# A four-layer graph kernel: layer 2 in the natural order of rows, and 18 of layer 3's gather slots joined into six

## The chip, the cores and the metric

The kernel runs on one core of one Trainium2 chip. The metric is the device time of one execution in microseconds (us); lower is better. Before the change the median of three runs is 708.24 us (708.03 to 709.66).

## The reference

Four graph layers work on one feature matrix `x` (2708 rows of 128 numbers, float32) and one sparse adjacency matrix `adj` (2708 x 2708, the same for all). Each layer adds its result to `x` and normalises every row:

```python
x = layernorm(x + layer0(x, adj))   # signed attention
x = layernorm(x + layer1(x, adj))   # relu(D^-1/2 (A + I) D^-1/2 (x W^T + b))
x = layernorm(x + layer2(x, adj))   # softmax over neighbours; entries below 1 are masked by (adj - 1) * 1e9
x = layernorm(x + layer3(x, adj))
# layer 3, for all i, j:
#   messages[i, j] = gelu(x_i Ws + x_j Wd + b);  agg_i = sum_j adj[i, j] * messages[i, j]
#   h = gelu([x_i, agg_i] Wu + bu) + x_i;  then a row norm with weights
```

Because of the mask, layer 2 needs of every row only its own (diagonal) entry and its largest neighbour. Layer 3 needs all non-zero neighbours of a row: up to some twenty, most rows far fewer.

## The kernel before, in words

The 2708 rows are 22 blocks of 128 (`NB`), one row per partition. While layers 0 and 1 run as dense products on TensorE (PE), VectorE (DVE) finds the non-zero entries of each row: their values in `V[row, block, slot]`, largest first, and their columns, from which `LIDX` is made. For that, rows are put into *places*: sorted by their number of neighbours, most first. `PERM` gives the row of a place, `RANK` the place of a row. `CAPS` gives how many slots a block of places has, from 21 down to 2, 187 in all. So a block with a large cap is one in which a few rows need many slots.

**Layer 1** (`half_of`, L740, with `finish`, L628) multiplies block after block. A chunk of four blocks is finished in small steps (`yield`) that are laid between the products of the next: transposes, residual and sums (DVE, L641 and L649), squares (ScalarE, ACT, L257), three small steps on GpSimd (POOL, L261 to L263), norm (L267), transposes, projection for layer 2 (L678, L684). Then the block goes to DRAM twice: as `TA` in the order of rows (L687, one plain DMA per chunk) and as `TS` in the order of places (L693, one indirect DMA by `RANK` for each block, on POOL). In the last stretch (L781 to L803) the steps still open are driven on after each product, by `if layer or m % 2` (L786). `in_order_of_rows` (L505) turns a vector in the order of places into the order of rows by 22 small matmuls; it is used for `dinv` in layer 1 (L892).

**Layer 2** (L908 to L1081) works on places, in four sets of 6, 6, 6 and 4 blocks. POOL gathers each place's largest neighbour from `TA` into `ga` (L918, 22 indirect DMAs), SP loads the places' own rows from `TS` into `OWN` (L922). For each set, `own_scores`, `shares` and `rows2` run mostly on DVE, `squares` on ACT with a product on PE, `roots` on DVE; `rows3` makes `yd`, what a row gives as a neighbour in layer 3, and scatters it to `TD` in the order of rows (L1052, 22 indirect DMAs on POOL; `yd` has two buffers). `norm3` writes the rows themselves into `X3` (L1061), all sets at the end. In the loop of L1070, `roots` and `rows3` of a set come one set later than its `squares`.

**Layer 3** (L1087 on) takes the 22 blocks of places in the order `TURN`. For turn k: `gathers` (L1150) fetches one slot of 128 neighbours from `TD` with each indirect DMA, into `G` (four buffers); `terms` makes x Ws + b on PE; `messages` adds (DVE, L1179) and applies gelu (ACT, L1180 and L1181); `diagonals` makes for every slot a diagonal matrix of the weights `V` (ACT, L1171); `update` multiplies message by diagonal and sums over slots in PSUM (PE, through `product`, L1143), then the update product and gelu (L1196); `added` and `norms` finish rows on DVE (L1206, L1217 to L1241); `stores` scatters them to the output (L1250, indirect DMA on POOL). Ahead of turn 0, `conditions` (L1099) tests whether the lists are complete and sets the flag that would call a dense path.

The order is written out by hand: `pinned` (L210) ties an instruction to the one pinned before it on the same engine. The DMAs of SP and ACT and the output stores are not pinned.

```python
def pinned(i):
    e = i.ins.engine
    if e in newest:
        tc.add_manual_dep(i.ins, newest[e].name, ..., reason="order")
    newest[e] = i.ins
    return i
```

Of the kernel before, what the change touches and what calls it, by code (L numbers as in the profile page):

```python
# [24 lines left out]
F32 = mybir.dt.float32  # L25
# [4 lines left out]
U32 = mybir.dt.uint32  # L30
# [20 lines left out]
TABLE = (("kk", 32), ("lane", 128), ("part", 1), ("lt", 128), ("ident", 128))  # L51


def table():
# [9 lines left out]
        "ident": p == np.arange(P),  # L64
    }
# [4 lines left out]
def sparse_path(  # L70
# [64 lines left out]
    TAB = const.tile([P, sum(w for _, w in TABLE)], F32, name="TAB")  # L135
    nc.scalar.dma_start(TAB, consts)
    part, at = {}, 0
    for name, w in TABLE:
        part[name] = TAB[:, at : at + w]
        at += w  # L140
# [62 lines left out]
    PERMF = const.tile([P, NB], F32, name="PERMF")  # L203

# [97 lines left out]
    def parts(dst, src, pool, n):  # L302

        rest = pool.tile([P, n], F32, name=f"rest{n}")
        nc.vector.tensor_copy(dst[:, :, 0], src)
        nc.vector.tensor_tensor(rest, src, dst[:, :, 0], ALU.subtract)
        nc.vector.tensor_copy(dst[:, :, 1], rest)
        nc.vector.tensor_tensor(rest, rest, dst[:, :, 1], ALU.subtract)
        nc.vector.tensor_copy(dst[:, :, 2], rest)
# [195 lines left out]
    def in_order_of_rows(ps, dst, src):  # L505

        s3 = small.tile([P, NB, 3], BF16, name="back3")
        parts(s3, src, small, NB)
# [89 lines left out]
    TS = dram.tile([NP, W_], F32, name="TS")  # L598
    H2 = lists.tile([P, NB, D], F32, name="H2")
    with (  # L600
# [27 lines left out]
        def finish(layer, bs, sT):  # L628
# [40 lines left out]
            if layer:  # L669
# [21 lines left out]

                for b in bs:
                    i = G_.indirect_dma_start(  # L693
                        TS, bass.IndirectOffsetOnAxis(ap=RANK[:, b : b + 1], axis=0),
                        XD[:, b, :], None,
                    )
                    tc.declare_no_dep(i.ins, group="TS", reason="each row has a place of its own")
                    tc.add_to_no_dep_group("TS", i.ins)
# [41 lines left out]
        def half_of(layer, h, weights, each, end, later):  # L740
# [40 lines left out]
            for i, c in enumerate(half):  # L781
                for m, (n, a) in enumerate(last):
# [3 lines left out]
                    if layer or m % 2:  # L786
                        for g in drain:
                            next(g, None)
# [79 lines left out]
        EARLY = 4  # L868
        for k in range(4):
            features(k)  # L870
        given(range(EARLY))
        weights(0)
        for h in range(2):

            def each1(n, a, lo, hi, h=h):
                if h:
                    return
# [28 lines left out]
    OWN = late.tile([P, NB, W_], F32, name="OWN")  # L906
    X3 = late.tile([P, NB, D], F32, name="X3")
    with (  # L908
# [6 lines left out]
        for k, bs in enumerate(sets):  # L915
            ga = gas[k] = one.tile([P, len(bs), D + HEADS], F32, name=f"ga{k}")
            for i, b in enumerate(bs):
                pinned(G_.indirect_dma_start(  # L918
                    ga[:, i, :], None, TA, bass.IndirectOffsetOnAxis(ap=LIDX[:, b, 0:1], axis=0)
                ))  # L920
        for k, bs in enumerate(sets):
            nc.sync.dma_start(  # L922
                OWN[:, bs[0] : bs[-1] + 1, :],
# [875 lines left out]
```

## Time and profile before

| what | value |
|---|---|
| median of three runs | 708.24 us |
| the profiled execution, its own time | 709.3 us |
| its span, first to last instruction | 707.5 us |
| mean granted TensorE clock | 0.766 |
| busy: PE, DVE, ACT, POOL | 451.2, 393.0, 272.4, 378.5 us |
| layer 3's gathers L1150 (POOL) | 187, mean 948 ns |
| layer 2's gathers L918 (POOL) | 22, mean 1075 ns |
| TS scatters L693, TD scatters L1052 (POOL) | 22 and 22, means 982 and 1102 ns |

The profile is one execution. A line of a timeline gives the start in us from the span's start, the duration, the engine, the line of the program, the operation with out<-in, and in brackets how long the engine sat idle before it and what ended that. A line of the costliest groups gives the busy time and the mean in ns, then the idle time before them with what ended most of it. "issue" is time for which the profile shows no wait. The digits of an engine's row in the part with 40 slices are tenths of busy time, each slice being 17.7 us. [...]

### The profile page before, as it was taken

Reading aid. Unit: us, or ns where it says so; the run is one execution under the profiler, and the core shown is the slowest. Engines: PE = TensorE matmul, PEld = TensorE weight load, DVE = VectorE, ACT = ScalarE, POOL = GpSimd, SP = SyncE. Lnnn points to the kernel's source line nnn. Section 1 sums busy time; section 2 is a strip of 40 time slices with the busy share of each in tenths; the row PEclk is TensorE's granted clock in tenths of the full one; section 3 lists DMA queues with packets and bytes.
Section 4 is the critical chain, followed back from the end, with each engine's and each line's share of the span. In section 5 each row is a group of like instructions: output and inputs, shape, how many; then the busy total and the mean of one; then the engine's idle time right before and its main releaser. Section 6 shows DMA issues by size and latency. Waiting matters only on the chain.

```text
span 707.5 us, 8193 instructions
## 1 busy us (share of the span) xinstructions
PE 451.2 (64%) x2565; PEld 301.7 (43%) x2565; DVE 393.0 (56%) x1138; ACT 272.4 (38%) x719; POOL 378.5 (53%) x449
## 2 busy tenths in 40 slices
PE   5889999996164999997511502066646546747461
PEld 5745445663152444464311501055536435545451
DVE  4767999999983856640208834111171251434466
ACT  3145655772330100174411574055335424444330
POOL 7002001221246776036577677777777777777761
PEclk9579999998556999999755555566776857788665
DMA  9968999996294999875254111222122122211210
GB/s 296 406 245 309 415 415 379 324 374 224 101 386 153 419 418 415 311 216 191 85 181 128 42 52 40 53 54 52 52 53 55 53 53 53 53 52 52 54 48 13
DMA packets 44400, 128.68 MB, mean 182 GB/s; under 512 B 7983, under 2 KB 19523, under 8 KB 38716
## 3 DMA queue, kind: packets, MB, share of 16 engines
q0 software_dynamic: 16832, 75.13, 30.2%
q1 hardware_dynamic: 21116, 49.66, 19.7%
q10 hardware_dynamic: 6400, 3.29, 1.7%
q8 instruction: 22, 0.36, 0.2%
q14 instruction: 30, 0.25, 0.1%
HBM read 119.29 MB, written 8.81 MB: 181 GB/s over the span
## 4 chain that ended last, share of the span: by engine, by line
DVE 27%; POOL 24%; PE 19%; issue 14%; DMA 9%; ACT 6%; SPq 0%; POOLq 0%; DVEq 0%; ACTq 0%
POOL G L1150 17%; PE acc L753 12%; DVE IX L580 9%; DVE cand L565 5%; DMA G<-TD,LIDX 4%; PE z L753 3%; POOL ga L918 2%; DMA TOP<-in_high 1%; POOL TS L693 1%; ACT squares L257 1%; PE w_ps L355 1%; ACT XD L267 1%; ACT X L1061 1%; DMA nat<-in_adjo,PERM 1%; POOL ln_r L262 1%
## 5 line engine op out<-in xcount | busy, mean ns | idle before, releaser
L1150 POOL DMA_INDIRECT G<-TD,LIDX x187 | 177.4, 948 | 58.7 <-issue 52.4
L1143 PE MATMUL aT_ps<-W,M 128*128 128x128 f32 x418 | 91.0, 394 | 112.5 <-ACT M L1180 105.1
L1143 PEld LDWEIGHTS aT_ps<-W,M 128*128 128x128 f32 x418 | 80.9, 292 | 126.4 <-ACT M L1180 114.0
L1179 DVE TENSOR_TENSOR M<-G,sd_ps 128x1152 f32<-128x1152 f32 (+11 forms) x22 | 28.3, 1287 | 159.0 <-DMA G<-TD,LIDX 142.8
L753 PE MATMUL acc<-ah,XD 128*128 128x512 f32 (+1 forms) x264 | 113.7, 568 | 1.0 <-ACT XD L626 1.0
L580 DVE FIND_INDEX8 IX<-V,nat 128x8 uint32<-128x2707 f32 x33 | 97.8, 2970 | 0.0
L830 ACT ACTIVATE sign<-ah 128x1536 bf16<-128x1536 f32 (+1 forms) x44 | 57.7, 1327 | 37.1 <-issue 26.8
L753 PE MATMUL acc<-ah,HS 128*128 128x512 f32 x132 | 63.3, 615 | 12.1 <-ACT HS L866 12.1
L753 PEld LDWEIGHTS acc<-ah,XD 128*128 128x128 f32 x264 | 47.9, 196 | 44.5 <-issue 41.4
L536 POOL DMA_INDIRECT nat<-in_adjo,PERM x22 | 21.5, 979 | 81.5 <-DVE IX L580 55.4
L1171 ACT ACTIVATE W<-TAB,V 128x128 f32<-128x128 f32 x187 | 56.8, 390 | 0.0
L558 DVE MAX8 V<-nat 128x8 f32<-128x2707 f32 x12 | 35.7, 2976 | 26.6 <-DMA nat<-in_adjo,PERM 26.6
L1180 ACT ACTIVATE M<-sd_ps 128x128 f32<-128x128 f32 x22 | 6.1, 278 | 113.2 <-DVE M L1179 113.2
L753 PEld LDWEIGHTS acc<-ah,HS 128*128 128x128 f32 x132 | 25.4, 196 | 44.7 <-issue 29.3
L866 ACT ACTIVATE HS<-HS,DS 128x128 f32<-128x128 f32 x22 | 8.4, 399 | 78.0 <-DMA HS<-TH,PERM 48.8
L565 DVE MAX8 cand<-nat 128x8 f32<-128x338 f32 (+3 forms) x88 | 34.3, 461 | 2.8 <-DMA nat<-in_adjo,PERM 2.8
L251 POOL TENSOR_SCALAR ln_a<-SUM 128x4 f32<-128x4 f32 (+1 forms) x12 | 2.9, 238 | 61.1 <-DVE XD L649 33.2
L1250 POOL DMA_INDIRECT out_x<-yo,PERM x22 | 22.1, 1003 | 18.5 <-DVE yo L1229 11.3
L861 POOL DMA_INDIRECT HS<-TH,PERM x22 | 21.0, 957 | 19.6 <-DMA TH<-H 10.1
L1052 POOL DMA_INDIRECT TD<-yd,PERM x22 | 24.2, 1102 | 9.6 <-ACT yd L1048 4.1
L753 PE MATMUL acc<-ah,H 128*128 128x512 f32 (+1 forms) x88 | 28.1, 462 | 0.0
L693 POOL DMA_INDIRECT TS<-XD,RANK x22 | 21.6, 982 | 11.3 <-issue 5.4
(281 smaller groups left out, 862.6 us busy)
## 6 DMA issues: line engine op xcount, KB each, us to landing
ah<-in_adjL SPq DMA_DIRECT2D x22, 768.0 KB, 13.5
ah<-in_adjR SPq DMA_DIRECT2D x44, 330.0 KB, 5.5
TOP<-in_high SPq DMA_DIRECT2D x5, 1354.0 KB, 13.0
ah<-in_adjL SPq DMA_DIRECT2D x22, 256.0 KB, 7.2
G<-TD,LIDX POOLq DMA_INDIRECT x187, 2.5
OWN<-TS SPq DMA_DIRECT2D x3, 798.0 KB, 8.5
TA<-XD ACTq DMA_DIRECT2D x5, 264.0 KB, 2.8
TH<-H ACTq DMA_DIRECT2D x5, 256.0 KB, 10.2
```

The source lines that it names most:

```text
L558: pinned(nc.vector.max(V[:, b, 0:8], t))
L565: pinned(nc.vector.max(c[:, 8 * k : 8 * k + 8], t[:, at]))
L580: pinned(nc.vector.max_index(IX[:, b, s], V[:, b, s], t))
L693: i = G_.indirect_dma_start(TS, bass.IndirectOffsetOnAxis(ap=RANK[:, b : b + 1], axis=0), XD[:, b, :], None,)
L753: pinned(T_.matmul(acc[i][:, :w], weights[:, n, :], a[:, i * BANK : i * BANK + w], start=n == 0, stop=n == NB - 1,))
L830: pinned(S_.activation(m[:, : hi - lo], a, AF.Sign))
L1052: i = G_.indirect_dma_start(TD, bass.IndirectOffsetOnAxis(ap=PERM[:, b : b + 1], axis=0), yd[:, i, :], None)
L1143: pinned(T_.matmul(t, a, b, start=n == 0, stop=n == len(parts) - 1))
L1150: pinned(G_.indirect_dma_start(G[:, s, :], None, TD, bass.IndirectOffsetOnAxis(ap=LIDX[:, b, s : s + 1], axis=0),))
L1171: pinned(S_.activation(W[:, s, :], ident, AF.Copy, scale=V[:, b, s : s + 1]))
L1179: pinned(V_.tensor_tensor(M[:, :n, :], G[:, :n, :], s_, ALU.add))
L1250: i = G_.indirect_dma_start(out, bass.IndirectOffsetOnAxis(ap=PERM[:, b : b + 1], axis=0), h, None, bounds_check=N - 1, oob_is_err=False,)
```

## The change

Layer 2 now works on rows in their natural order. `OWN` is the tile `XD` that layer 1 leaves in SBUF; `TS`, its scatters and its load are gone. The two vectors that layer 2 needs of the lists, the largest neighbour's value (`V1`) and its column (`J1`), are brought into the order of rows by `in_order_of_rows` in the second half of layer 1, at blocks 5 and 9. `TD` is written by a plain DMA on SP for each set. What layer 3 needs in the order of places (the rows, the diagonal and the count: 130 numbers) is scattered by `RANK` to `XS` (`to_places`, 22 indirect DMAs on POOL, pinned) and read back into `X3S` (`from_places`, four DMAs on SP). In layer 2's loop `roots` and `rows3` follow the `squares` of the same set. In layer 1's last stretch the open steps are not driven on during the last, short chunk.

In layer 3, 18 slots that few rows use are joined into six groups (`JOINED`: block, slot, number of rows). Each group is one gather of at most 128 rows (`joined_gathers`), with a message step of its own; its indices and weights are collected by 36 small DMAs on SP (`joined_lists`). In `update` a block uses its piece of a group through a shifted part of the identity. `FULL` is what is left of `CAPS`: 169 slots, none in block 21. `conditions` counts with a mask (`uses`). The `XJ` memset is on DVE. In `messages` the own row's gelu now comes ahead of DVE's add.

```diff
@@ -48,7 +48,42 @@
 CAPS = (21, 13, 12, 11, 11, 10, 10, 9, 9, 9, 8, 8, 8, 7, 7, 6, 6, 6, 5, 5, 4, 2)
-TABLE = (("kk", 32), ("lane", 128), ("part", 1), ("lt", 128), ("ident", 128))
+JOINED = (
+    ((2, 11, 97), (0, 16, 23), (0, 20, 8)),
+    ((1, 12, 85), (0, 15, 41)),
+    ((0, 14, 65), (17, 5, 62)),
+    ((20, 3, 68), (19, 4, 48), (9, 8, 12)),
+    ((6, 9, 56), (4, 10, 41), (0, 17, 14), (0, 18, 10)),
+    ((12, 7, 40), (21, 0, 26), (21, 1, 22), (0, 19, 9)),
+)
+FULL = tuple(
+    min([c] + [s for q in JOINED for b, s, _ in q if b == k]) for k, c in enumerate(CAPS)
+)
+PARTS = tuple(
+    tuple(
+        (q, sum(m for *_, m in g[:i]), n)
+        for q, g in enumerate(JOINED)
+        for i, (b, _, n) in enumerate(g)
+        if b == k
+    )
+    for k in range(len(CAPS))
+)
+def used(b, s):
+    if s >= CAPS[b]:
+        return 0
+    return next((n for g in JOINED for k, t, n in g if (k, t) == (b, s)), P)
...
                     TA[bs[0] * P : (bs[-1] + 1) * P, :].rearrange("(b p) c -> p b c", p=P),
                     XP[:, g, : D + HEADS],
                 )
...
-                for b in bs:
-                    i = G_.indirect_dma_start(
-                        TS, bass.IndirectOffsetOnAxis(ap=RANK[:, b : b + 1], axis=0),
-                        XD[:, b, :], None,
-                    )
-                    tc.declare_no_dep(i.ins, group="TS", reason="each row has a place of its own")
-                    tc.add_to_no_dep_group("TS", i.ins)
...
@@ -783,7 +814,7 @@
                     product(n, a, i)
                     if not layer:
                         search(0.28)
-                    if layer or m % 2:
+                    if m % 2 if not layer else c != NC - 1:
                         for g in drain:
                             next(g, None)
...
             def each1(n, a, lo, hi, h=h):
                 if h:
+                    if n == 5:
+                        in_order_of_rows(pt, V1, V[:, :, 0])
+                    if n == 9:
+                        pinned(V_.tensor_copy(JF, LIDX[:, :, 0]))
+                        in_order_of_rows(pt, JS, JF)
+                        pinned(V_.tensor_copy(J1, JS))
                     return
...
+    USES = late.tile([P, NB, SLOTS], F32, name="USES")
+    nc.sync.dma_start(USES.rearrange("p b s -> p (b s)"), consts[:, W_TAB:])
+    NJ = len(JOINED)
+    LJ = late.tile([P, NJ], U32, name="LJ")
+    VJ = late.tile([P, NJ], F32, name="VJ")
+    nc.gpsimd.memset(LJ, 0)
+    nc.gpsimd.memset(VJ, 0.0)
+    def joined_lists():
+        for q, g in enumerate(JOINED):
+            at = 0
+            for b, s, n in g:
+                nc.sync.dma_start(LJ[at : at + n, q : q + 1], LIDX[:n, b, s : s + 1])
+                nc.sync.dma_start(VJ[at : at + n, q : q + 1], V[:n, b, s : s + 1])
+                at += n
+    OWN = XD
+    X3N = late.tile([P, NB, D + 2], F32, name="X3N")
+    X3S = late.tile([P, NB, D + 2], F32, name="X3S")
+    X3 = X3S[:, :, :D]
+    XS = dram.tile([NP, D + 2], F32, name="XS")
+    def to_places(bs):
+        for b in bs:
+            i = pinned(G_.indirect_dma_start(
+                XS, bass.IndirectOffsetOnAxis(ap=RANK[:, b : b + 1], axis=0), X3N[:, b, :], None
+            ))
+            tc.declare_no_dep(i.ins, group="XS", reason="each row has a place of its own")
+            tc.add_to_no_dep_group("XS", i.ins)
+    def from_places():
+        for bs in groups(6):
+            nc.sync.dma_start(
+                X3S[:, bs[0] : bs[-1] + 1, :],
+                XS[bs[0] * P : (bs[-1] + 1) * P, :].rearrange("(b p) c -> p b c", p=P),
+            )
...
             ga = gas[k] = one.tile([P, len(bs), D + HEADS], F32, name=f"ga{k}")
             for i, b in enumerate(bs):
                 pinned(G_.indirect_dma_start(
-                    ga[:, i, :], None, TA, bass.IndirectOffsetOnAxis(ap=LIDX[:, b, 0:1], axis=0)
+                    ga[:, i, :], None, TA, bass.IndirectOffsetOnAxis(ap=J1[:, b : b + 1], axis=0)
                 ))
-        for k, bs in enumerate(sets):
-            nc.sync.dma_start(
-                OWN[:, bs[0] : bs[-1] + 1, :],
-                TS[bs[0] * P : (bs[-1] + 1) * P, :].rearrange("(b p) c -> p b c", p=P),
-            )
+        pinned(V_.tensor_copy(X3N[:, :, D:], DD))
...
         pinned(V_.tensor_tensor(LIDX[:, :, 1:], j, up, ALU.add))
+        joined_lists()
...
         AM = one.tile([P, NB, 2], F32, name="AM")
-        pinned(V_.tensor_scalar(AM[:, :, 1], V[:, :, 0], 1.0, MASK, ALU.subtract, ALU.mult))
+        pinned(V_.tensor_scalar(AM[:, :, 1], V1, 1.0, MASK, ALU.subtract, ALU.mult))
...
                     pinned(S_.activation(
                         yd[:, lo + i, :], z[:, i, :], AF.Copy, scale=t[:, 3, lo + i : lo + i + 1]
                     ))
-            for i, b in enumerate(bs):
-                i = G_.indirect_dma_start(
-                    TD, bass.IndirectOffsetOnAxis(ap=PERM[:, b : b + 1], axis=0), yd[:, i, :], None
-                )
-                tc.declare_no_dep(i.ins, group="TD", reason="each row has a place of its own")
-                tc.add_to_no_dep_group("TD", i.ins)
+            nc.sync.dma_start(
+                TD[bs[0] * P : (bs[-1] + 1) * P, :].rearrange("(b p) d -> p b d", p=P),
+                yd[:, : len(bs), :],
+            )
...
         def norm3(k):
             zs, t = mid[k]
             for i, b in enumerate(sets[k]):
                 pinned(S_.activation(
-                    X3[:, b, :], XO[:, b, :], AF.Identity, bias=t[:, 0, i : i + 1],
+                    X3N[:, b, :D], XO[:, b, :], AF.Identity, bias=t[:, 0, i : i + 1],
                     scale=t[:, 3, i : i + 1],
                 ))
...
         shares(0)
         for k in range(last + 1):
             rows2(k)
+            squares(k)
             if k < last:
                 shares(k + 1)
-            squares(k)
-            if k:
-                roots(k - 1)
-                rows3(k - 1)
-        roots(last)
-        rows3(last)
-        for k in range(last + 1):
+            roots(k)
+            rows3(k)
+            if k < last - 1:
+                norm3(k)
+                to_places(sets[k])
+        for k in (last - 1, last):
             norm3(k)
+        to_places(sets[last - 1])
...
         pinned(V_.tensor_tensor(W3[:, D : 2 * D], W3[:, :D], WD, ALU.add))
-        pinned(V_.tensor_tensor(X3B, X3, LN_B.unsqueeze(1).to_broadcast([P, NB, D]), ALU.add))
...
             has = one.tile([P, NB, SLOTS], F32, name="has")
-            pinned(V_.tensor_scalar(has, V, 0.0, None, ALU.is_gt))
+            pinned(V_.scalar_tensor_tensor(has, V, 0.0, USES, ALU.is_gt, ALU.mult))
             count = one.tile([P, NB], F32, name="count")
-            for b in range(NB):
-                pinned(V_.tensor_reduce(count[:, b : b + 1], has[:, b, : CAPS[b]], AX.X, ALU.add))
-            pinned(V_.tensor_tensor(count, count, OWN[:, :, W_ - 1], ALU.not_equal))
+            pinned(V_.tensor_reduce(count, has, AX.X, ALU.add))
+            pinned(V_.tensor_tensor(count, count, X3S[:, :, D + 1], ALU.not_equal))
             pinned(V_.tensor_reduce(FL[:, 4:5], count, AX.X, ALU.max))
...
-            pinned(V_.tensor_tensor(gap, V[:, :, 0], OWN[:, :, W_ - 2], ALU.max))
+            pinned(V_.tensor_tensor(gap, V[:, :, 0], X3S[:, :, D], ALU.max))
...
+        GJ = one.tile([P, NJ, D], F32, name="GJ")
+        XJ = one.tile([P, NJ, P], F32, name="XJ")
+        def joined_gathers():
+            for q in range(NJ):
+                pinned(G_.indirect_dma_start(
+                    GJ[:, q, :], None, TD, bass.IndirectOffsetOnAxis(ap=LJ[:, q : q + 1], axis=0)
+                ))
+            pinned(V_.memset(XJ, 0.0))
+        def joined_rows():
+            for b in range(NB):
+                if PARTS[b]:
+                    t = ps.tile([P, P], F32, name="xT_ps")
+                    pinned(T_.transpose(t, X3[:, b, :], ident))
+                    for q, at, n in PARTS[b]:
+                        pinned(S_.copy(XJ[:, q, at : at + n], t[:, :n]))
+        def joined_messages():
+            for q in range(NJ):
+                m = ps.tile([P, 2 * D], F32, name="sd_ps")
+                product(m[:, :D], ((ONES, BIAS[:, :D]), (XJ[:, q, :], W3[:, :D])))
+                pinned(V_.tensor_tensor(GJ[:, q, :], GJ[:, q, :], m[:, :D], ALU.add))
+                pinned(S_.activation(GJ[:, q, :], GJ[:, q, :], AF.Gelu))
         def gathers(k):
             b = TURN[k]
-            n = CAPS[b]
-            G = Gs[k] = gp.tile([P, CAPS[0], D], F32, name="G")
+            n = FULL[b]
+            if not n:
+                return
+            G = Gs[k] = gp.tile([P, FULL[0], D], F32, name="G")
             for s in range(n):
                 pinned(G_.indirect_dma_start(
                     G[:, s, :], None, TD,
@@ -1162,30 +1260,52 @@
             product(m, ((ONES, BIAS[:, : 2 * D]), (xT, W3[:, : 2 * D])))
             mids[k] = m, xT
...
         def diagonals(k):
             b = TURN[k]
-            n = CAPS[b]
-            W = Ws[k] = wp.tile([P, CAPS[0] + 1, P], F32, name="W")
+            n = FULL[b]
+            W = Ws[k] = wp.tile([P, FULL[0] + 1 + len(PARTS[0]), P], F32, name="W")
+            for i, (q, at, m) in enumerate(PARTS[b]):
+                pinned(S_.activation(
+                    W[:, n + 1 + i, :m], shifted(at, m), AF.Copy, scale=VJ[:, q : q + 1]
+                ))
             for s in range(n):
                 pinned(S_.activation(W[:, s, :], ident, AF.Copy, scale=V[:, b, s : s + 1]))
-            pinned(S_.activation(W[:, n, :], ident, AF.Copy, scale=OWN[:, b, W_ - 2 : W_ - 1]))
+            pinned(S_.activation(W[:, n, :], ident, AF.Copy, scale=X3S[:, b, D : D + 1]))
         def messages(k):
-            n = CAPS[TURN[k]]
-            G, m = Gs.pop(k), mids[k][0]
-            M = Ms[k] = wp.tile([P, CAPS[0] + 1, D], F32, name="M")
-            s_ = m[:, :D].unsqueeze(1).to_broadcast([P, n, D])
-            pinned(V_.tensor_tensor(M[:, :n, :], G[:, :n, :], s_, ALU.add))
+            n = FULL[TURN[k]]
+            m = mids[k][0]
+            M = Ms[k] = wp.tile([P, FULL[0] + 1, D], F32, name="M")
             pinned(S_.activation(M[:, n, :], m[:, D : 2 * D], AF.Gelu))
-            pinned(S_.activation(M[:, :n, :], M[:, :n, :], AF.Gelu))
+            if n:
+                G = Gs.pop(k)
+                s_ = m[:, :D].unsqueeze(1).to_broadcast([P, n, D])
+                pinned(V_.tensor_tensor(M[:, :n, :], G[:, :n, :], s_, ALU.add))
+                pinned(S_.activation(M[:, :n, :], M[:, :n, :], AF.Gelu))
         def update(k):
-            n = CAPS[TURN[k]]
+            n = FULL[TURN[k]]
             i, j = place[k]
             M, W, xT = Ms.pop(k), Ws.pop(k), mids.pop(k)[1]
             t = ps.tile([P, P], F32, name="aT_ps")
-            product(t, [(M[:, s, :], W[:, s, :]) for s in (n, *range(n))])
+            own = [(t, M[:, n, :], W[:, n, :])]
+            all_ = [(t, M[:, s, :], W[:, s, :]) for s in range(n)]
+            some = [
+                (t[:, :m], GJ[:, q, :], W[:, n + 1 + i_, :m])
+                for i_, (q, at, m) in enumerate(PARTS[TURN[k]])
+            ]
+            todo = own + some + all_ if n else own + some
+            for i_, (to, x_, w_) in enumerate(todo):
+                pinned(T_.matmul(
+                    to, x_, w_, start=i_ == 0, stop=i_ == len(todo) - 1, skip_group_check=True
+                ))
...
+        joined_gathers()
         gathers(0)
+        to_places(sets[last])
+        from_places()
+        pinned(V_.tensor_tensor(X3B, X3, LN_B.unsqueeze(1).to_broadcast([P, NB, D]), ALU.add))
         conditions()
+        joined_rows()
+        joined_messages()
         terms(0)
         diagonals(0)
```

Left out: the table's new column block and its load, the pinned form of `parts`, and the declarations of `V1`, `J1`, `JF` and `JS`.

## Prediction

> **What bounds the kernel now.** I read the page first: busy shares, the slices, the costliest groups.
>
> ```profile
> span 707.5 us, 8193 instructions
> ...
> PE 451.2 (64%) x2565; PEld 301.7 (43%) x2565; DVE 393.0 (56%) x1138; ACT 272.4 (38%) x719; POOL 378.5 (53%) x449
> ...
> POOL 7002001221246776036577677777777777777761
> ...
> L1150 POOL DMA_INDIRECT G<-TD,LIDX x187 | 177.4, 948 | 58.7 <-issue 52.4
> ...
> L1052 POOL DMA_INDIRECT TD<-yd,PERM x22 | 24.2, 1102 | 9.6 <-ACT yd L1048 4.1
> ```
>
> POOL is 53% busy overall, but from slice 24 to the end it never rests: 187 gathers of 0.948 us, each with 0.30 us of "issue" before it, so 1.25 us apiece. From 428.8 to 687.7 nothing else paces the kernel. So two things count: when that stream starts, and how many items it has. The timeline of POOL shows the first.
>
> ```profile
> 361.64 0.96 POOL L693 DMA_INDIRECT TS<-XD,RANK  x1 [0.30 <-issue]
> 362.90 1.00 POOL L918 DMA_INDIRECT ga<-TA,LIDX  x1 [0.30 <-issue]
> ...
> 423.52 3.23 POOL L1052 DMA_INDIRECT TD<-yd,PERM  x1 [0.30 <-DMA TD<-yd,PERM]
> 428.80 1.29 POOL L1150 DMA_INDIRECT G<-TD,LIDX  x1 [2.05 <-DVE odd L1110]
> 430.39 0.96 POOL L1150 DMA_INDIRECT G<-TD,LIDX  x1 [0.30 <-issue]
> ```
>
> Layer 2's gathers queue behind the TS scatters (362.9), the stream behind the TD scatters (the DVE named at 428.80 does not feed the gather; the last scatter's landing does). The timelines of DVE and ACT say what layer 2 waits for.
>
> ```profile
> 369.64 0.17 DVE L962 TENSOR_SCALAR AM<-OWN 128x6 f32<-128x6 f32 x1 [15.96 <-DMA OWN<-TS]
> ...
> 377.91 0.18 DVE L974 TENSOR_TENSOR E<-ga,OWN 128x24 f32<-128x24 f32 x1
> ```
>
> ```profile
> 413.23 1.14 ACT L1048 ACTIVATE yd<-d_ps,sums 128x128 f32<-128x128 f32 x4 [2.96 <-DMA TD<-yd,PERM]
> ```
>
> DVE idles 15.96 us for OWN; shares(0) begins at 377.91; the last yd waits 2.96 us for a buffer the scatters still read. Last, DVE at the end of layer 3:
>
> ```profile
> 647.33 0.95 DVE L1179 TENSOR_TENSOR M<-G,sd_ps 128x768 f32<-128x768 f32 x1 [5.83 <-DMA G<-TD,LIDX]
> ...
> 659.58 0.82 DVE L1179 TENSOR_TENSOR M<-G,sd_ps 128x640 f32<-128x640 f32 x1 [0.42 <-DMA G<-TD,LIDX]
> ...
> 674.52 0.29 DVE L1206 TENSOR_TENSOR yo<-yo,X 128x128 f32<-128x128 f32 x1 [1.97 <-ACT yo L1196]
> ```
>
> At turn 17 the gathers are only 0.42 us late: there DVE's norms nearly bind. After 674.52 the end (33.0 us) is a DVE chain that no gather holds.
>
> **Part 1: the end of layer 1.** Removed: 22 TS scatters (1.26 us each on POOL). Eight of them (334.7 to 344.6) hold ln_a of chunk 4, whose sums were ready at 343.3: 1.3 us. Earlier they hold ln_v at 321.99 and 330.8, behind which PE idles 2.49 and 1.36 us. The last six (355.2 to 362.6) hold the layer 2 gathers. Added: two conversions to row order (V1, J1). The one that is there (dinv) costs DVE 2.66 us from 290.01 and PE 0.86 us. DVE has gaps for them; PE, in order, may wait for the second, 0 to 3.2 us. So PE: +1.7 for the two, +0 to 3.2 waiting, -3.85 of stalls gone; bounds -3 and +3, and I take 0. If DVE had no gaps each would cost 2.7 us.
>
> The changed drain puts chunk 5's products and its copy ahead of chunk 4's finish, so the two finish together. From chunk 4's copy at 340.0 with the old durations: adds, relus and sums to 345.2; squares (six of 0.39) to 347.3; POOL's pow (1.05 and 0.71) to 349.7; norms to 350.9; transposes and copies to 352.3; products and copies to 355.4; TA's second issue 355.8 (358.32 before), landed near 358.2. With nothing left on POOL the ga gathers start at **358.0**, not 362.9.
>
> **Part 2: layer 2.** Own rows are now read from XD; the OWN load and its wait are gone, and own_scores (5.7 us of DVE) ends by 359, under the gathers. shares(0) needs six gathers: 6 x 1.26, and 2 to 3.2 us to landing (ga's median is 3.2): 367.5, not 377.9. Call it T.
>
> From here the loop is serial, which is a cost: roots(k) now comes before rows2(k+1). One round is rows2 4.1 (379.56 to 383.68), squares 2.4, roots 2.25, about 9 us; the gathers give a set per 7.6, so the loop paces. rows2(0) starts at T+1.7, but rows2(1) at T+12 because shares(1) must have its gathers; rows2(2) T+21, rows2(3) T+29.8 (3.2 long, four blocks), squares(3) to T+34.8, roots(3) T+37.2, yd(3) T+38.5, norm3(2) first row T+39. The TD writes are plain DMAs on SP: TA's of the same size land in 2.8 us, so TD is whole by T+41.5, in place of 22 scatters of 1.1 us. But POOL first has 6 scatters of set 2, from T+39.1: 6 x 1.26 to **T+46.7 = 414.2**. POOL's own sum is no later: 358 + 22 x 1.26 + 18 x 1.26 = 408.4, plus about 3 for gathers that meet a two-input add. Such gathers take 1.33 to 1.41 us here (379.12, 384.91) against 0.94. The Trainium skill ("SBUF — State Buffer", section "Who interferes with whom") says tensor_tensor was not seen to stall DMA issue; by it POOL is free at 408.4, by the trace near 411.5. I use the trace. With 0.8 for what SP's small copies may add, the stream starts at **S = 415**, 13.8 us sooner.
>
> **Part 3: 36 list copies on SP.** They gather the joined indices and weights, 4 bytes per row, from 353.5 (LIDX ready). SP's TD writes queue behind them. Nearest rows: POOL's 4-byte loads (AJI) issue 0.51 us apart and overlap; ACT's TA issues take 0.37. 36 x 0.5 = 18 us, done at 372, under the gathers; TD is needed at 409. A rule speaks against this: the skill ("DMA: Bandwidth & Descriptors", section "Why a DMA increments its semaphore by 16 and not by 1") says a DMA uses the largest k up to 16 that divides its slowest dimension, so 97, 23 or 41 rows go to one engine. By that one engine gets some 584 of the 1454 pieces. The small-packet row (q10: 6400 packets, 1.7% of 16 engines) gives 0.03 us a packet: 17.5 us; at twice that, 35 us, done at 389. Both are hidden, so I take the row, 0. Below zero is excluded: nothing was there before.
>
> **Part 4: layer 3.** POOL from S to turn 16's last gather: before, 165 gathers; now 152 + 6 joined, and 4 scatters of set 3 (1.26). -7 x 1.25 + 5.05 = **-3.7** us. (The other 5 removed slots lie in turns 17 to 21.)
>
> Turn 0 now has a longer run-up, all hidden if POOL keeps going. Set 3's scatters end at S + 7.5 + 17.5 + 5.05 = S+30; landing 2.7 (TS): S+33; X3S in four loads (OWN, twice as big, took 12.4 from first issue to the last wait): S+40; X3B 3.1, conditions 7.6 (22 reduces become one): S+51; joined rows, 18 copies at 0.22: S+55; six joined messages on PE, DVE, ACT, near 0.9 each: S+60; terms and the first add (14 x 128, 2.0): S+64. POOL asks for that buffer when it reaches gathers(4), the fifth tile of four: S + 7.5 + 17.5 + 5 + 34 x 1.25 = S+73. Slack 9. Afterwards a turn costs about 8 us (490.56 to 498.38 for 12 slots) against POOL's 12.5 to 15, so the lag is gone by turn 7. PE's work is unchanged in count (418 matmuls, some narrower). The XJ memset, mask load and copies lie in DVE's and SP's idle time.
>
> Turns 17 to 20 have 4, 5, 3, 5 gathers instead of 5, 6, 4, 5. DVE's norms hold turn 17's add at 11.8 us after turn 16's (12.25 before); the ACT-PE chain, 6.1 a turn, brings turn 18's added to 23.6, before 27.2: **-3.6**, not the -3.75 of the gathers alone. Then 33.0 us as before; turn 21 loses its two gathers, but they did not bind.
>
> **Sum.** -13.8 - 3.7 - 3.6 = -21.1. The profiled execution takes 709.3 (span 707.5 and 1.8 around it): 688.2. Against the median 708.24: **687.1**. Own range of this case 680 to 693: the conversions and T within 3 us each way, S within 3 more.
>
> **Rivals.**
> - *Joined work late.* If conditions, joined rows and messages take half as long again, the first add comes near S+80 and POOL waits some 7 us for a G buffer: 694. For it: PE's clock is 0.5 around 400 and each step is a handover. Against: 9 us of slack. Chance 0.12.
> - *Layer 2 keeps its pace.* ACT's squares, copies, yd and norm3 (7.5 us a set) sit in the loop; if a round costs 4 us more, three rounds put S at 427: 699. Against: every duration is a row. Chance 0.08.
> - *Slower: SP's list copies run one after another.* If each pays the skill's fixed 2.0 us (same page, section "Anatomy of one DMA — SWDGE (gpsimd) path", given there for POOL's DMAs) plus an issue of 0.4, they end at 353.5 + 36 x 2.4 = 440, the last TD write lands at 442.7, S is 27.7 later: 714.8. It decides from about 2.2 us a copy, where S meets 436. Against: the AJI rows overlap. Chance 0.07.
>
> **Numbers.** Forecast 0.73, then 0.12, 0.08, 0.07. About 0.3% is what a measurement of this kernel can tell from no change. Faster 0.73 + 0.12 + 0.08 = 0.93; the third rival, near its deciding point, leaves 0.02 for the same and 0.05 for slower. The range 680 to 699 takes in the forecast's own and the first two rivals.
>
> **What would show it.** First ga near 358; shares(0) near 367.5 with no OWN wait; 18 XS scatters on POOL without a gap over 2 us, ended near 415; TD whole before that; SP's list copies done by 390; no idle POOL before gathers(4); gathers 175; turn 18's added 23.6 us after turn 16's add. It is wrong if POOL waits inside the stream, if the joined gathers wait for TD, or if chunk 4's copy moves more than 3 us.

## The result, and the profile after

The changed kernel takes 701.77 us (median of 5 runs, 699.34 to 702.02), the kernel before beside it 708.03 us: ratio 0.990, 95% interval 0.988 to 0.992. The prediction was 687.1 us, 680 to 699: the direction holds, two thirds of the gain are missing. Its own profiled execution took 701.77 us, with a span of 699.5.

The page after, the same rows as before:

```profile
span 699.5 us, 8404 instructions
...
PE 439.9 (63%) x2644; PEld 298.4 (43%) x2644; DVE 397.2 (57%) x1144; ACT 274.6 (39%) x742; POOL 347.5 (50%) x417
...
POOL 7001000321154866312147757787777777777731
...
L1248 POOL DMA_INDIRECT G<-TD,LIDX x169 | 163.2, 966 | 51.5 <-issue 45.7
```

POOL is busy 31 us less (378.5 before), and the span is only 8 us shorter. The stream is as dense as before. The last but one digit of POOL's row is 3, not 6: the end is now mostly wait.

POOL's timeline after, at the places shown of before. An indirect DMA keeps POOL busy for 0.94 us as a rule; its data land 2.5 us after the issue (the median of the messages' gathers):

```profile
363.20 1.11 POOL L994 DMA_INDIRECT ga<-TA,J  x1 [9.00 <-DMA VJ<-V]
...
412.79 0.96 POOL L971 DMA_INDIRECT XS<-X3N,RANK  x1 [4.51 <-ACT X3N L1132]
...
416.59 0.98 POOL L971 DMA_INDIRECT XS<-X3N,RANK  x1 [1.57 <-ACT X3N L1132]
...
422.97 0.99 POOL L1220 DMA_INDIRECT GJ<-TD,LJ  x1 [0.30 <-issue]
...
460.65 3.74 POOL L1248 DMA_INDIRECT G<-TD,LIDX  x1 [0.30 <-issue]
```

The layer 2 gathers start at 363.20 (362.90 before, 358.0 predicted), the stream at 422.97 (428.80; 415). Between lie two waits for X3N, and inside the stream one gather of 3.74 us that the prediction did not have. DVE for layer 2, at the X3B add (which the held gather outlasts by 0.8 us) and at turn 18, then ACT (ACTq is ACT's issue of a DMA):

```profile
372.50 0.18 DVE L1047 TENSOR_TENSOR E<-ga,XD 128x24 f32<-128x24 f32 x1 [12.34 <-DMA ga<-TA,J]
...
460.49 3.09 DVE L1381 TENSOR_TENSOR X3B<-X3S,LN_B 128x2816 f32<-128x2816 f32 x1 [43.61 <-DMA X3S<-XS]
...
661.48 0.28 DVE L1326 TENSOR_TENSOR yo<-yo,X3S 128x128 f32<-128x128 f32 x1
```

```profile
343.47 0.59 ACT L822 COPY sT<-acc 128x512 f32<-128x512 f32 x1 [3.05 <-PE acc L784]
...
359.17 0.37 ACTq L726 DMA_DIRECT2D TA<-XD  x1
...
410.99 1.14 ACT L1121 ACTIVATE yd<-d_ps,sums 128x128 f32<-128x128 f32 x4 [2.17 <-PE d_ps L1103]
412.01 3.95 ACT L1132 ACTIVATE X3N<-XD,sums 128x128 f32<-128x128 f32 x10
```

The copy at 343.47 is chunk 4's, with which the finish of chunk 4 begins (340.02 before); the last write of TA is issued at 359.17. The wait for OWN is gone, shares(0) is at 372.50 (367.5 predicted), the last yd 38.5 us after it, as predicted; ten rows of X3N follow it on ACT from 412.01 to 415.96. Turn 18's added is at 661.48, 13.0 us sooner than before.

Last, the end. The last store starts 13.5 us sooner (702.44 to 688.97), but the span ends only 8.0 sooner. The view of the line that closes the program shows why. It gives the engine, the operation, its number, and the least, median and longest duration in ns; of before, then of after:

```profile
L1790 POOLq DRAIN  x3: 46/115/3312, 703.4 to 707.2; - x3
```

```profile
L1916 POOLq DRAIN  x3: 46/115/8809, 689.9 to 699.3; - x3
```

POOL's drain behind the last store takes 8.81 us, not 3.31. The program's end waits for it.

On the chip of the first four runs below (e1 to e4) every kernel is slow in layer 3, the kernel before at 785 us, so of these runs only the drains and the traces up to some 360 us are used, and e2 to e4 were run again on another chip as e2b, e3b and e4b.

### The profile page after: what moved, and what is told of

The parts are those of the page before. It is cut to its first block, busy times and chain, and to the rows that moved or that the text cites. A ratio compares the mean times of both kernels' runs of the same rounds, so it can differ in the third digit from the quotient of the medians.

```text
span 699.5 us, 8404 instructions
## 1 busy us (share of the span) xinstructions
PE 439.9 (63%) x2644; PEld 298.4 (43%) x2644; DVE 397.2 (57%) x1144; ACT 274.6 (39%) x742; POOL 347.5 (50%) x417
## 5 line engine op out<-in xcount | busy, mean ns | idle before, releaser
L1248 POOL DMA_INDIRECT G<-TD,LIDX x169 | 163.2, 966 | 51.5 <-issue 45.7
L1306 PE MATMUL aT_ps<-W,M 128*128 128x128 f32 x382 | 70.0, 347 | 70.2 <-ACT M L1290 69.7
L1306 PEld LDWEIGHTS aT_ps<-W,M 128*128 128x128 f32 x382 | 64.8, 252 | 75.0 <-ACT M L1290 73.0
L1289 DVE TENSOR_TENSOR M<-G,sd_ps 128x1152 f32<-128x1152 f32 (+10 forms) x21 | 25.7, 1226 | 103.7 <-ACT M L1285 51.5
L784 PE MATMUL acc<-ah,HS 128*128 128x512 f32 x132 | 63.5, 618 | 13.3 <-ACT HS L897 13.3
L598 DVE MAX8 V<-nat 128x8 f32<-128x2707 f32 x12 | 35.7, 2976 | 27.5 <-DMA nat<-in_adjo,PERM 27.5
L1278 ACT ACTIVATE W<-TAB,V 128x128 f32<-128x128 f32 x169 | 51.3, 386 | 0.0
L1290 ACT ACTIVATE M<-M 128x1152 f32<-128x1152 f32 (+10 forms) x21 | 22.3, 1061 | 67.4 <-DVE M L1289 67.4
L892 POOL DMA_INDIRECT HS<-TH,PERM x22 | 21.0, 956 | 20.0 <-DMA TH<-H 10.2
L994 POOL DMA_INDIRECT ga<-TA,J x22 | 22.4, 1020 | 15.4 <-DMA VJ<-V 9.0
L971 POOL DMA_INDIRECT XS<-X3N,RANK x22 | 22.3, 1014 | 12.2 <-ACT X3N L1132 6.7
```

Of the source, the lines that this page charges most:

```text
L598: pinned(nc.vector.max(V[:, b, 0:8], t))
L784: pinned(T_.matmul(acc[i][:, :w], weights[:, n, :], a[:, i * BANK : i * BANK + w], start=n == 0, stop=n == NB - 1,))
L971: i = pinned(G_.indirect_dma_start(XS, bass.IndirectOffsetOnAxis(ap=RANK[:, b : b + 1], axis=0), X3N[:, b, :], None))
L994: pinned(G_.indirect_dma_start(ga[:, i, :], None, TA, bass.IndirectOffsetOnAxis(ap=J1[:, b : b + 1], axis=0)))
L1248: pinned(G_.indirect_dma_start(G[:, s, :], None, TD, bass.IndirectOffsetOnAxis(ap=LIDX[:, b, s : s + 1], axis=0),))
L1278: pinned(S_.activation(W[:, s, :], ident, AF.Copy, scale=V[:, b, s : s + 1]))
```

## The experiments

Theory: the layer 2 part gives little because each of its gains met a wait (PE's stall on the last conversion, X3N behind yd on ACT, the X3B add inside the stream) and the end grew by the drain. Rivals: the joined work is what falls short; or the list copies hold TA and the first gathers back.

**Which part brings what.** e3 and e3b: layer 2 alone.

```diff
-JOINED = (((2, 11, 97), (0, 16, 23), (0, 20, 8)), ...)
+JOINED = ()
...
-        joined_gathers()
         gathers(0)
```

> The measured terms, against the kernel before: the stream starts 5.8 us sooner, 3 scatters in it cost 3.8, the X3B add's hold 2.8, the time behind the last store 5.4 more if it comes with this part: 714; 708.5 if it does not. By the prediction's terms (stream 13.8 sooner, 4 scatters 5.05) it would be 699.5. If the list copies held TA or the ga gathers back, the first ga gather comes 1 to 2 us before 363.2.

> As e3. The joined gathers alone gave 694.0 where the changed kernel takes 699.3 and before 708.1: if the two parts add up, layer 2 alone costs 5.3, of which 5.6 is the longer wait behind the last store; e3's own trace had the short wait (2.34), so 707 to 709, no change. By the prediction's terms (stream 13.8 sooner, 4 scatters 5.05 in it) it would be 699.5.

e4 and e4b: the kernel before with the joined gathers alone (its layer 2 in places, its TS and TD scatters, `LJ` and `VJ` from the same 36 list copies; the shorter `conditions` and the new order in `messages` are in it too).

```diff
+        joined_gathers()
         gathers(0)
         conditions()
+        joined_rows()
+        joined_messages()
```

> By the prediction's terms: 7 items of 1.25 us fewer up to turn 16 (-8.75) and -3.6 (measured -5.2) in the last turns: 694 to 695.7. If the longer time behind the last store comes with this part, 5.4 more: 699.5 to 701. If the list copies on SP delay the OWN loads, shares(0) comes after 377.9 and the time is higher by as much.

> As e4: 694 to 695.7 where before takes 708, by the prediction's own terms for the joined gathers, and a wait behind the last store of 2.3 to 3.3 us and not 8.8. If it is no faster than the changed kernel, the gain of the joined gathers depends on layer 2.

And the changed kernel again, beside e4b, e5 and e6:

> The changed kernel itself, as the yardstick beside the others. If the chip gives the kernel before some 708 us again: 700 to 702, 0.99 of it. If layer 3 is slow again as in the first four runs (before at 785): PE's wait of 3.43 on back_b, the first ga gather near 360 and the 8.81 us wait behind the last store should be there, since e2 showed all three; the ratio near that of e2, 1.00.

| kernel | us, median (range) | ratio to before, 95% | drain, us |
|---|---|---|---|
| e3 (first chip) | 784.7 (783.0 to 785.8) | 1.000 (0.998 to 1.001) | 2.34 |
| e3b layer 2 alone | 707.36 (705.98 to 709.86) | 0.998 (0.996 to 1.000) | 2.29 |
| e4 (first chip) | 772.82 (770.98 to 782.61) | 0.984 (0.981 to 0.987) | 2.98 |
| e4b joined alone | 693.96 (693.33 to 701.01) | 0.983 (0.977 to 0.989) | 2.87 |
| changed kernel again | 699.29 (697.08 to 699.88) | 0.987 (0.985 to 0.990) | 8.81 |

The joined gathers alone are worth the 12.35 us that the prediction gave them (8.75 to turn 16, 3.6 behind it: 695.7); the 1.7 more lie within the interval, some 4 us to each side. Layer 2 alone, for which it had 8.75 (13.8 less 5.05), is worth about 1.5 us, and on top of the joined gathers the median is 5.3 us worse. The drain accounts for all of that: it is long in neither part alone (2.29 and 2.87) and 8.81 in both together, 5.9 more than in e4b. Up to the last store the two together are ahead, 684.28 against 687.07 in the profiled executions of the changed kernel (2.2 us under its median) and of e4b. The rival on the joined work falls. In e3b the stream starts at 421.54, 7.3 us sooner than before, and its last store at 700.57, 1.9 sooner: 3 scatters in the stream (3.8) and a gather of 3.86 us under the X3B add (2.9 more than usual) are 6.7, more than the 5.4 between; where 1.3 were won back is not shown. The list copies fall too: without them the first ga gather starts 4.25 us (e3) and 3.84 us (e3b) after TA's last issue, with them 4.03 (profile after) and 3.74 (again). The timeline names VJ as what ended that wait; the runs show that it isn't what binds.

**The stall of the conversion.** e1 puts the TensorE half of J1's conversion off.

```diff
                     if n == 9:
                         pinned(V_.tensor_copy(JF, LIDX[:, :, 0]))
-                        in_order_of_rows(pt, JS, JF)
-                        pinned(V_.tensor_copy(J1, JS))
+                        in_order_of_rows(pt, JS, JF, pending)
+                    if n == 13:
+                        in_order_end(pt, *pending.pop())
+                        pinned(V_.tensor_copy(J1, JS))
```

> Theory (the stall on back_b is on the path): the 3.43 us wait of PE at 321.7 and the slow matmuls behind it go, chunk 4's copy falls from 343.5 back to about 340, the first ga gather from 363.2 to 359.8, and the time from 701.8 to 698.4. Rival (the end of layer 1 is held by the finish chain of ACT and POOL, not by PE): chunk 4's copy comes early but the first ga gather moves less than 1 us, time 701 to 702.

Against e2 on the same chip, whose layer 1 is that of the changed kernel, chunk 4's copy falls from 340.24 to 335.88 and the first ga gather from 360.06 to 355.64: 4.4 us. The theory holds; the time (781.14 us, ratio 0.994, 0.992 to 0.996) counts for less there. The same edit in e6 (below) brings chunk 4's copy to 336.89. PE's timeline shows the wait in the profile after, and then in the changed kernel run again (in e6 no wait on back_b is left):

```profile
321.72 1.40 PE L556 MATMUL q_ps<-back_b,BACK 128*128 128x66 bf16 x22 [3.43 <-DVE back_b L551]
322.92 2.16 PE L717 MATMUL q_ps<-W,xt 128*128 128x136 f32 x8
```

```profile
321.28 0.87 PE L556 MATMUL q_ps<-back_b,BACK 128*128 128x66 bf16 x22 [3.44 <-DVE back_b L551]
321.99 1.21 PE L717 MATMUL q_ps<-W,xt 128*128 128x136 f32 x8
```

The stall is the same in the two, but what follows is not: 8 products take 2.16 us in one and 1.21 in the other. The table by stretch tells it for these two runs. A row gives the stretch and its length, the busy us and number of instructions of PE, PEld (PE's weight loads), DVE, ACT and POOL, then the granted clock, and last the DMA share and GB/s:

```profile
324.00:328.00 4.00, 4.00 (x14) 2.95 (x14) 0.00 (x0) 2.31 (x10) 0.79 (x2) 0.51 0.00 0
```

```profile
324.00:328.00 4.00, 4.00 (x26) 3.04 (x25) 1.93 (x12) 3.88 (x15) 1.95 (x5) 1.00 0.67 161
```

Behind the same idle time the clock was 0.51 in one execution and 1.00 in the other; chunk 4's copy came at 343.47 and 340.37. Seven of the profiled executions have this stall, of 3.43 to 3.45 us. The 8 products took 2.16 us in three (the profile after, e2b, e3b), 1.75 in e3 and 1.21 in three (again, e2, e5), and the copy came at 342.2 to 343.5, 341.2, and 340.0 to 340.4. It may be a part of the changed kernel's spread from run to run. The profile of before has such a place too, which the prediction did not read:

```profile
317.33 2.38 PE L753 MATMUL acc<-ah,H 128*128 128x512 f32 x8
...
324.23 1.54 PE L664 MATMUL o_ps<-TAB,XD 128*128 128x128 f32 x4 [2.49 <-ACT XD L267]
325.57 4.06 PE L753 MATMUL acc<-ah,H 128*128 128x512 f32 x8
```

```profile
324.00:328.00 4.00, 3.59 (x9) 2.00 (x10) 0.00 (x0) 3.90 (x15) 1.96 (x3) 0.69 0.41 137
```

Behind 2.49 us of idle time 8 products took 4.06 us, not 2.38; from 326 to 328 the clock was 0.50. The Trainium skill ("TensorE: Matmul & The Clock Gate", section "What's actually happening") gives a free-running window of 3.413 us, and the half clock after at least one idle window. That a stall of 3.43 us has two outcomes would fit, if it counts where in the window it begins; but the 2.49 us of before are shorter than the window, so here an idle time need not fill it. What decides is not shown.

**The idle POOL ahead of the joined gathers.** e5 writes X3N of each set right behind its yd, and scatters all four sets ahead of the joined gathers.

```diff
             rows3(k)
-            if k < last - 1:
-                norm3(k)
-                to_places(sets[k])
-        for k in (last - 1, last):
             norm3(k)
-        to_places(sets[last - 1])
+            to_places(sets[k])
...
         gathers(0)
-        to_places(sets[last])
```

> Theory (POOL's idle 4.51 and 1.57 us ahead of the joined gathers are lost, because norm3 of set 2 stands behind yd of set 3 on ACT): scatters of set 2 start near 409 right behind those of set 1, POOL idles under 2 us in all between 392 and the joined gathers, 4 to 6 us gained: 696 to 698. Rival (ACT is the bound of the layer 2 loop): norm3 of set 2 pushes squares and yd of set 3 back by 2.4 us, TD is whole 2.4 us later and the joined gathers wait for it: gain under 2, 700 or more.

693.14 us (691.83 to 697.02), ratio 0.980 (0.976 to 0.985), 6.15 less than the changed kernel beside it; with four runs each that is good to some 3 us, and the last store of the profiled executions comes 5.0 us sooner (684.28 to 679.26). POOL's timeline:

```profile
409.85 0.97 POOL L971 DMA_INDIRECT XS<-X3N,RANK  x1 [0.30 <-ACT X3N L1132]
...
417.49 0.98 POOL L1216 DMA_INDIRECT GJ<-TD,LJ  x1 [0.30 <-issue]
...
427.54 3.26 POOL L1244 DMA_INDIRECT G<-TD,LIDX  x1 [0.30 <-issue]
```

The 22 scatters follow each other without a gap, most of them 1.27 us apart, and the joined gathers start 2.1 us sooner (417.49 against 419.56) although all of set 3 is now ahead of them: with the 3 scatters that left the stream (3.8) that makes 5.9. The last yd came 39.1 us after shares(0), 38.5 in the changed kernel beside it: ACT had the room, and the rival falls. The changed kernel had 4.51 us of idle there, and 1.57 before the third scatter of the group, which starts 0.6 us after the last of the ten X3N rows is written. Besides, its trace has 19 scatters ahead of the joined gathers where the program's text has 18, and 3 in the stream where it has 4: in the built program one of set 3 stands ahead. If it is the third of the group, that explains the 1.57; the trace does not name the row.

**The X3B add.** e2 and e2b cut it into 22.

```diff
-        pinned(V_.tensor_tensor(X3B, X3, LN_B.unsqueeze(1).to_broadcast([P, NB, D]), ALU.add))
...
             messages(k)
+            for b in TURN[2 * k : 2 * k + 2]:
+                pinned(V_.tensor_tensor(X3B[:, b, :], X3[:, b, :], LN_B, ALU.add))
```

> Theory (a long two-input add holds one gather back for its whole length): no gather near 460 lasts over 1.5 us, POOL gains 2.8 us less what 22 small adds of about 0.28 us take back: 699 to 701. Rival (the port time is what counts, not the length of one add): the small adds take back all, 702 to 704, seen as a higher mean of the gathers (966 ns now).

> As e2, where the changed kernel takes 699.3: by the theory (one gather is held 1.75 to 2.8 us by the X3B add) 696.5 to 698; by the rival (the small adds take it back) 699 to 700, with a higher mean of the gathers.

e2b takes 699.21 us (697.68 to 699.89), ratio 0.986 (0.983 to 0.989), as the changed kernel (699.29). The long gather is gone, and the 169 gathers of messages take 160.9 us instead of 161.8, while the 22 adds take DVE 5.4 us instead of 3.1; nothing of that can be told in the time. e2 (787.7 us, ratio 1.003, 1.001 to 1.005) says nothing more. The hold is real: in seven traces (before, after, again, e3b, e4b, e5, e9) the indirect DMA that meets this add ends 0.81 to 0.84 us after it. Its price in time is not shown.

**The drain.** e6 is the three edits together with 8 memsets of 4 bytes a partition on POOL, e7 the same with 40, e8 without memsets and with 14 idle gathers at the kernel's start, all into one tile. In e9, e10 and e11 (split conversion and norm3 early, X3B in one add) 8, 4 and 12 idle gathers, whose data nobody reads, stand behind the last message gather:

```diff
                 gathers(k + 1)
+                if k == NB - 2:
+                    for q in range(8):
+                        pinned(G_.indirect_dma_start(
+                            more[:, q, :], None, TD,
+                            bass.IndirectOffsetOnAxis(ap=LIDX[:, q, 0:1], axis=0),
+                        ))
```

> The three edits together (split conversion -3.4, norm3 early -5, X3B in pieces -2.8 to 0): 690 to 693, if they lie one behind the other on the path. Eight tiny memsets on POOL change its instruction count and not its count of indirect DMAs: if the 8.81 us wait behind the last store comes from where POOL's instructions lie, it falls to about 3 and the time to 685 to 688; if it comes from the indirect DMAs, it stays at 8.81.

> e6 with 40 tiny memsets on POOL in place of 8, so that it has more instructions (513) than the kernel before (505) and as few indirect DMAs as the changed kernel (327). If the 8.8 us wait behind the last store depends on the number or the place of POOL's instructions, it is 2.3 to 3.3 now and the time 683 to 685; if on the indirect DMAs, it stays 8.8 and the time 689 to 691.

> e6 without the memsets and with 14 idle gathers of 64 KB on POOL in the first microseconds of the kernel, so 341 indirect DMAs in the program (327 in the changed kernel and in e6; 339, 349, 361 in e3, e4 and before, where the wait behind the last store was short). If the 8.8 us wait comes with the number of indirect DMAs, it is short now, and the time 683 to 685, plus what the early gathers cost; if not, it stays.

> Split conversion and norm3 early, X3B in one add, no memsets, and 8 idle gathers (each into a tile column of its own, read by nobody) on POOL behind the last message gather: 335 indirect DMAs in the program. If the drain's 8.8 us comes from a number of indirect DMAs below a bound under 335, it is 2.3 to 3.3 and the time 683 to 685; if the bound lies above 335, 689. The idle gathers take 10 us of the 11.4 that POOL waits there, so nothing else should move.

> As e9 with 4 idle gathers: 331 indirect DMAs. 683 to 685 with a short drain, 689 with a long one. If the drain is long here and short in e9, the change lies between; if its length is neither 8.8 nor about 2.5, it grows with the distance from a bound.

> As e9 with 12 idle gathers: 339 indirect DMAs, as in e3, where the drain was short. By the count theory: short drain, and up to 3 us more than the best of e9 and e10, since 12 x 1.25 = 15 us is more than the 11.4 us that POOL waits there: 685 to 688. If the drain is long (689 or more), the number of indirect DMAs is not what decides.

The count is of all DMAs that POOL issues, 20 plain ones among them:

| kernel | DMAs on POOL | drain, us | us, median (range) | ratio to before, 95% |
|---|---|---|---|---|
| changed kernel, e1, e2, e2b, e5 | 327 | 8.81 to 8.82 | | |
| e6 | 327 | 8.80 | 689.07 (688.80 to 690.29) | 0.973 (0.970 to 0.976) |
| e7 | 327 | 8.80 | 688.97 (687.17 to 689.69) | 0.973 (0.970 to 0.975) |
| e10 | 331 | 9.44 | 690.98 (690.37 to 691.52) | 0.974 (0.971 to 0.976) |
| e9 | 335 | 2.14 | 686.83 (683.73 to 687.31) | 0.968 (0.966 to 0.970) |
| e11 | 339 | 2.61 | 689.36 (688.61 to 690.15) | 0.971 (0.969 to 0.973) |
| e3, e3b | 339 | 2.34, 2.29 | | |
| e8 | 341 | 2.45 | 715.17 (714.52 to 715.82) | 1.009 (1.006 to 1.012) |
| e4, e4b | 349 | 2.98, 2.87 | | |
| before | 361 | 3.31 | | |

The view of the closing line again, of e9:

```profile
L1928 POOLq DRAIN  x3: 46/115/2137, 678.5 to 681.5; - x3
```

e6 is 10.2 us under the changed kernel beside it, which fits the 4.4 of the conversion and the 6.15 of the order. The other instructions on POOL don't matter (e6, e7), and four more idle gathers turn a drain of 9.44 us into 2.14. So the long drain goes with the number of DMAs that POOL issues in these programs, long to 331 and short from 335. It grows from 327 (8.80) to 331 (9.44), falls, and is longer again at 361 (3.31) than at 335 (2.14), which speaks against a plain threshold. Why is not shown.

What the shorter drain is worth is shown in part only. e9's is 6.7 us shorter than e6's, and its median only 2.2 us less (686.83, where 683 to 685 were expected). In its profile, which is of its fastest run, POOL also rests 2.53 us ahead of its last store ("issue", 1.05 <-DVE in the changed kernel), and its runs lie near 684 and 687: something of the wait may have moved rather than gone. e11's 12 idle gathers push the stores back, by a little more than expected. e8's gathers into one tile waited for each other, 4.2 to 6.8 us from one to the next, and put the whole kernel back by 26 us against e6; only its drain is of use.

e9 is the best version: 3.2% under the kernel before, and 15 us under the changed kernel's 701.8, which stood beside other runs of before.

## Why the prediction was wrong

The predicted sum gives a span of 707.5 - 21.1 = 686.4; the measured one is 699.5, 13.1 us more. T is the start of shares(0), S that of the stream. By the prediction's own steps:

- **"PE: ... bounds -3 and +3, and I take 0" (part 1).** The step failed in the profiled execution and held in another: chunk 4's copy at 343.47 and 340.37 against 340.0. Its "0 to 3.2" of waiting is 3.43 and 3.44; with the wait taken away the copy comes at 336.9. The term for the clock behind a stall was missing on both sides: 3.1 us when it falls behind the new stall, and some 1.7 us (4.06 for 2.38) that went with the old stall of 2.49 beside its length. So where the step held, the second made up for a wait at the top of its bounds, by luck. **+3.5.**
- **"TA's second issue ..., landed near 358.2", gathers at 358.0.** Mis-sized: 2.2 us from the last issue to the first gather, which is even less than its own landing of 2.4; measured 4.03, and 3.74 to 4.25 in the runs above. It is not the list copies. What makes it longer than the 2.8 us that TA's writes took before (the median) is not shown. **+1.8.**
- **shares(0) 9.5 us behind the first gather**: measured 9.30. Right.
- **"POOL first has 6 scatters of set 2, from T+39.1: 6 x 1.26 to T+46.7".** The loop ended as predicted to 0.1 us (last yd at T+38.5), but T to S took 50.5 us in place of 47.5. The first scatter came at T+40.3 (+1.2), the third waited 1.3 us more than the usual 0.30 (+1.3), a seventh scatter stood in the group (+1.3), and the 0.8 for SP's copies was not needed. **+3.0.** The sum also passed over a contradiction of its own: its times leave POOL nothing to do from 401 or 404 (408.4 or 411.5 less six scatters) until T+39.1 = 406.6, yet it expected no gap over 2 us. It took this wait for X3N as given, where it came from the order on ACT, norm3 of set 2 behind the last yd: in e5, with another order, S comes 48.8 us after T with all 22 scatters ahead of it, and the time is 6.15 us less.
- **Part 3, the list copies free.** Right: 0.57 to 0.83 us each where it had 0.5, so done by 376 and not 372, but TD's writes from 386.8 were not held.
- **Part 4.** From S to turn 16's last gather 214.9 us, predicted 213.1 (216.8 before, less 3.7): the gather under the X3B add (+2.8) was missing, one scatter fewer lay inside (-1.3), and 0.3 are left over. For these gathers I had used the trace's 1.33 to 1.41 us under an add of 0.95, but did not look for the longest add that meets the stream. The prediction even shows such a row, the TD scatter of 3.23 us at 423.52, which lies under the X3B add of before (422.83 to 425.92). The statement of the Trainium skill weighed there ("SBUF — State Buffer", section "Who interferes with whom", on tensor_tensor and DMA issue) is again not borne out, now by 3.74 us for 0.94; another bullet of the same section, that a DVE instruction with two SBUF inputs contends with a GpSimd instruction that reads SBUF, is the one that fits. The run-up was right (first add at S+63.5, no wait for a buffer); turns 17 and 18 gave 5.2 us, not 3.6. Together from S to the last store: 266.0 us, predicted 266.3. **-0.3**, errors that cancel.
- **"33.0 us as before".** Right up to the last store (27.5 us from turn 18's added, 27.9 before), wrong behind it: 10.5 us to the end of the span, 5.1 before. **+5.4**, the largest single term. It was put at no change without a reason: the sum never asked what the program does behind its last store, which in the profile of before is a drain of 3.31 us and after is one of 8.81. Why it grew stays open; it goes with the number of POOL's DMAs.

Sum: 3.5 + 1.8 - 0.2 (shares(0)) + 3.0 - 0.3 + 5.4 = 13.2, the 13.1 but for rounding. Outside the span the execution took 2.3 us, predicted 1.8.

Of the rivals, "layer 2 keeps its pace" came nearest in time (699), for a wrong reason: no round of the loop got slower. "SP's list copies run one after another" is excluded. That the end could grow was no rival of mine.

## What to carry to other kernels

Work that leaves an engine's queue shortens the kernel only if what follows in that queue is ready: for each item behind the removed ones, ask for its input's time, and where it is late, whether another order on the engine that makes it would bring it sooner. Test the parts of a double change apart: here one part had nearly all the gain, and the two together had a long end that neither has alone. Look at what the program does behind its last store, and keep idle times of PE short where it sets the pace: the clock behind them cost up to 3.1 us here, for a stall of 3.43.

## What the runs showed of the hardware that was not expected

- POOL's last drain takes 8.8 to 9.4 us in the programs where POOL issues 327 and 331 DMAs, and 2.1 to 3.3 us in those with 335 and more.
- One two-input DVE add of 3.09 us over SBUF holds an indirect DMA on POOL for 3.74 us (0.94 otherwise); in seven traces it ends 0.81 to 0.84 us after the add.
- Idle time of 3.43 us on PE was followed by a granted clock of 0.51 in one execution and 1.00 in another of the same kernel, and idle time of 2.49 us by 0.50 in the kernel before.
